# A graph layer on one core: one-hot moved within the step, loads of targets and weights moved back, eight gathers in one group

## The chip, the cores and the metric

The kernel runs on one core of a Trainium2 chip. The metric is the device time of one execution in microseconds (us); less is better. The engines are TensorE (PE, with its weight loads shown as PEld), VectorE (DVE), ScalarE (ACT), GpSimd (POOL) and SyncE (SP). Here SP computes nothing: it issues most of the transfers, one after the other, from one queue. POOL issues the indirect ones.

## The reference, cut to what matters

```python
h = relu(layernorm(x))                        # x: 12500 x 128
msg_src = h @ w_src + b_src;  msg_dst = h @ w_dst
m = msg_src[src] + msg_dst[dst]               # 400000 edges, sorted by dst
rad = silu(silu(edge_attr @ w1 + b1) @ w2 + b2) @ w3 + b3    # 32 -> 64 -> 64 -> 128
m = m * edge_weight * rad
m = (m @ w_sep + b_sep).reshape(E, 8, 32)     # per head: 16 for alpha, 16 for the value
alpha = smooth_leaky_relu(m[:, :, :16]);  value = m[:, :, 16:]
score = einsum('ehk,hk->eh', alpha, alpha_dot)
att = segment_softmax(score, dst)             # over the edges with one target
out = segment_sum(value * att, dst).reshape(12500, 128)
y = x + out @ w_proj + b_proj
```

## The kernel before

**Node phase.** x is loaded in eight transfers. 25 quads of four tiles of 128 rows are then normalised, turned by PE, multiplied with both weight matrices (`products(i)`), copied out of PSUM by ACT (L261, tile `ms`, four buffers) and stored by SP to the tables `t_src` and `t_dst` in HBM (L266). The loop over the quads is written out in order (manual schedule). On SP's queue, between x and the first table store, stand the loads that the later phases need: the targets of all edges as `cur`, 125 rows of 3200 words, and the same shifted by one word as `prev` (L169 to L172); `base`, the first target of each section, in two transfers that repeat one row over the partitions (L176); `ends`, single words, the first and last target of each section (L177); and 14 loads of copies of the small weights in blocks (L188 to L194). 15 more weights are loaded by the helper `load` (L110) from ACT's queue.

At quad 12 `fits()` compares `prev` with `cur` to find out whether the targets are sorted, and from `ends` whether a section of 500 edges spans fewer than 64 targets. After the loop `cuts()` computes a row of marks `same`, where a target differs from the one before, stores it to HBM and makes some small tiles of weights.

**Step phase.** If all fits, `windows()` runs. It takes 1000 edges in a step k, two sections f = 0 and 1 of 500 edges (four tiles of 125). Work on one pair of sections is spread over many steps: loads and gathers run ahead of k, the sums follow in step c = k - 12, and a softmax scan over eight pairs runs once in eight steps. The order of each engine's instructions is the order in which the step's code is written. The parts that the text below speaks of:

- SP's loads: `w_b` (L713, edge weights repeated over 128 partitions), `md` (L719, rows of `t_dst`), `d_b` (L707), `e_t` (L702, edge attributes), the rows for `add_x`; and its stores: `sc_d` (L841, scores), `ob` to the row of `agg` of its window (L924).
- `gather(k, f)`, L739: four indirect transfers, issued by POOL, of 125 rows of `t_src` each, into a tile `gs0` or `gs1` with four buffers. A step issues `gather(k+4, 1)` in its first half and `gather(k+5, 0)` later.
- `prep_make` makes POOL's indices once in 16 steps, `split_md` the parts of md, `add_x` adds x to a chunk of the result in one step of eight.
- `mlp3(k)`: the third matmul of the radial net (L790), then `rad` on DVE (L794).
- `sources(k, f)`: four transposes (L803) of the gathered rows into PSUM (`pm0` or `pm1`).
- `message(k, rad)`: adds `msg_dst` by a one-hot matmul (L811) to `pm`, then mT = (pm + b) * rad on DVE (L816).
- `values(c, f)`: V = mT @ w_v (L901), then pvx = V * Pem, the weights of the softmax, on DVE (L903).
- `alphas(k, f)`: pa = w_a by mT (L820, one PSUM buffer), a sigmoid `sl` on ACT (L822), al = pa * sl on DVE (L824).
- `mlp1(k+2)` (L758), `mlp2(k+1)` (L773): the first two layers of the radial net.
- `sums_begin(c)`: copies the weights beside pvx (ACT), and makes `oh`, the one-hot of each edge's target in its window, on DVE (L888 and L891).
- `sums(c)`: the segment sums as matmuls of `oh` with `pvx` (L912), copied out by ACT as `ob` (L916).
- `e_T` (L749) and `scores` (L831) follow, `scores` in odd steps.

The order of PE's work in a step before: `mlp3(k)`, `sources(k, 1)`, `message(k)`, `values(c, 0)`, `alphas(k, 0)`, `mlp1(k+2)`, `values(c, 1)`, `sources(k+1, 0)`, `alphas(k, 1)`, `mlp2(k+1)`, `sums(c)`, `e_T`, `scores`. The one-hot is issued to DVE at the head of the step, before `rad`.

**The end.** The last 13 steps have only the sums of the pairs still under way. Then parts of windows are scattered, and a final phase multiplies the sums by w_proj and adds x.

Of the kernel before, what the change touches and what calls it, by code (L numbers as in the profile page):

```python
# [30 lines left out]
P = 128  # L31
C = 128
# [24 lines left out]
def gnn_kernel(ctx: ExitStack, tc: tile.TileContext, a: dict, out: bass.AP):  # L57
# [47 lines left out]
    ident = const.tile([P, P], F32, name="ident")  # L105
    make_identity(nc, ident)

    def load(name, shape, ap=None, eng=None):
        t = const.tile(shape, F32, name="c_" + name)
        (eng or nc.scalar).dma_start(out=t, in_=a[name] if ap is None else ap)  # L110
        return t

    eps = const.tile([P, 1], F32, name="eps")
    nc.vector.memset(eps, LN_EPS)
    ones = const.tile([P, P], F32, name="ones")
# [38 lines left out]
    with tc.tile_pool(name="node", bufs=2) as np_, tc.tile_pool(name="node1", bufs=1) as n1, \  # L154
# [9 lines left out]
        dst_r = dst.rearrange("(p c) -> p c", p=RP)  # L164
        cur = n1.tile([RP, RC], I32, name="cur")
        prev = n1.tile([RP, RC], I32, name="prev")
        ends = n1.tile([100, 8, 2], I32, name="ends")
        eb = n1.tile([P, NS, 2], I32, name="eb")
        nc.sync.dma_start(out=cur, in_=dst_r)  # L169
        nc.vector.memset(prev[0:1, 0:1], -1)  # L170
        nc.sync.dma_start(out=prev[0:1, 1:RC], in_=dst_r[0:1, 0:RC - 1])
        nc.sync.dma_start(out=prev[1:RP, :], in_=dst[RC - 1:E - 1].rearrange("(p c) -> p c", c=RC))  # L172
        at = dst[0:1]
        with nc.allow_non_contiguous_dma(reason="the sections' ends"):
            for f in range(2):
                nc.sync.dma_start(out=base[:, f, :], in_=dst_h[f:f + 1, :, 0])  # L176
            nc.sync.dma_start(out=ends, in_=bass.AP(  # L177
                at.tensor, at.offset, [[8 * SEC, 100], [SEC, 8], [SEC - 1, 2]]))
# [6 lines left out]
        for f in range(2):  # L185
            for q in range(2):
                o = (2 * q + f) * RAD
                nc.sync.dma_start(out=w1b[o:o + RAD, f * FC:(f + 1) * FC], in_=a["fc_w1"])  # L188
            s = slice(f * FC, (f + 1) * FC)
            for q in range(2):  # L190
                nc.sync.dma_start(out=w2b[s, q * FC:(q + 1) * FC], in_=a["fc_w2"])
            nc.sync.dma_start(out=w3b[s, :], in_=a["fc_w3"])
            nc.sync.dma_start(out=b12[s, 0:1], in_=a["fc_b1"])
            nc.sync.dma_start(out=b12[s, 1:2], in_=a["fc_b2"])  # L194
        b_n = load("b_n", [C, 1], a["b_src"].rearrange("o c -> c o"))
        dot = load("dot", [C, 1])
        heads = load("heads", [C, C])
        w1, b1 = load("fc_w1", [RAD, FC]), load("fc_b1", [FC, 1])
        w2, b2 = load("fc_w2", [FC, FC]), load("fc_b2", [FC, 1])
        w3, b3 = load("fc_w3", [FC, C]), load("fc_b3", [C, 1])  # L200
        w_a, b_a = load("w_a", [C, C]), load("b_a", [C, 1])
        w_v = load("w_v", [C, C])
        w_proj = load("w_proj", [C, C])
        b_out = load("b_out", [P, C], a["b_proj"].to_broadcast([P, C]))
        b_v = load("b_v", [C, 1])


        mv = n1.tile([P, NB, 2], F32, name="mv")
# [60 lines left out]


        def fits():
            gt = n1.tile([RP, RC], BF16, name="gt")
            nc.vector.tensor_tensor(gt, prev, cur, op=ALU.is_gt)
            cnt = n1.tile([P, 2], F32, name="cnt")
            nc.vector.memset(cnt, 0.0)
            nc.vector.tensor_reduce(cnt[:RP, 0:1], gt, AX.X, ALU.add)
# [24 lines left out]
        v_out = const.tile([P, C], F32, name="v_out")  # L301

        def cuts():
            sm = n1.tile([RP, RC], BF16, name="sm")
            nc.vector.tensor_tensor(sm, prev, cur, op=ALU.not_equal)
            nc.vector.tensor_scalar(sm, sm, RESTART, None, op0=ALU.mult)
            nc.sync.dma_start(out=same[:, 0:E].rearrange("o (p c) -> (o p) c", p=RP), in_=sm)
# [36 lines left out]

    chunks = [(t, min(CH, TPI - t)) for t in range(0, TPI, CH)]
# [310 lines left out]
    def windows():  # L656
# [5 lines left out]
        with tc.tile_pool(name="wk2", bufs=2) as sp, tc.tile_pool(name="ps", bufs=1, space=PSUM) as pp, \  # L662
                tc.manual_schedule(), ExitStack() as held:
            lp = held.enter_context(tc.tile_pool(name="ld", bufs=2))
            prep, e_g, d_g, w_g, md, gath = {}, {}, {}, {}, {}, {}
            eTs, h1s, h2s, ohT, m3, mr, mTs, als, S_all, sms, Ps, Pem, pvx, ohs, accs, xs, Ms, pms = (
                {} for _ in range(18))


            def prep_load(u):  # L670
# [60 lines left out]
                else:  # L731
                    nc.vector.tensor_sub(m3[k][:, 2, :], mr.pop(k), m3[k][:, 1, :])

            def gather(k, f):
                gs = lp.tile([P, TS, C], F32, name=f"gs{f}", bufs=4)
                idx, _ = prep[k // 16]
                for j in range(TS):
                    t = k % 16 * 8 + f * TS + j
# [3 lines left out]
                gath[k, f] = gs  # L742


            def e_T(k):
# [49 lines left out]
                                                   op0=ALU.add, op1=ALU.mult)  # L795
                return rad

            def sources(k, f):

                gs = gath.pop((k, f))  # L800
                pms[k, f] = pp.tile([C, SEC], F32, name=f"pm{f}")
                for t in range(TS):
                    nc.tensor.matmul(pms[k, f][:, t * T:(t + 1) * T], gs[:T, t, :], ident[:T, :T],  # L803
                                     start=(t == 0), stop=False, is_transpose=True, skip_group_check=True)

            def message(k, rad):
                pm = [pms.pop((k, f)) for f in range(2)]
                for j in range(3):
                    for f in range(2):
                        s = slice(f * W, (f + 1) * W)  # L810
# [66 lines left out]
                nc.scalar.copy(Pem[m].rearrange("p t q h -> p t (q h)"), pt)  # L877


            def sums_begin(c):  # L880
                pvx[c] = sp.tile([T, 2, TS, ROW], F32, name="pvx")
                q = c % MP * 2
                for f in range(2):
                    nc.scalar.copy(pvx[c][:, f, :, C:ROW], Pem[c // MP][:, :, q + f, :])
                _, loc = prep[c // 16]
                ohs[c] = sp.tile([T, 8, W], F32, name="oh")
                t0 = c % 16 * 8
# [7 lines left out]

            def values(c, f):
                V = pp.tile([T, TS, C], F32, name="V") if c < NP - LAG else \
                    pp.tile([T, TS, C], F32, name=f"pm{f}")
# [42 lines left out]
            def has(k):  # L941
                return 0 <= k < NP
# [5 lines left out]
            def step(k):  # L948
# [377 lines left out]
```

## Time and profile before

| | before |
|---|---|
| median of three runs | 4723.23 us (4720.04 to 4723.61) |
| the profiled execution | 4712.63 us, span 4710.8 us |
| mean granted TensorE clock | 0.964 |
| busy, PE / PEld / DVE / ACT / POOL | 89% / 50% / 65% / 41% / 67% |
| moved by DMA | 796.36 MB, mean 169 GB/s |

The profile is that of one execution. A row of its groups or waits names a line of the kernel, an engine, an operation and its tiles (out<-in), how often, the busy time and the mean of one in ns, then the idle time just before and who ended it. A row of a timeline gives the start, the duration, engine, line and operation, and in brackets a wait and what ended it. "SPq" is SP's queue, where the time between two issues is shown since SP has no busy time. A row of the view by windows gives a stretch of time, and then for each engine the busy time and the number of instructions in it, the granted clock, the share of the 16 DMA engines that was busy and GB/s.

### The profile page before, as it was taken

Reading aid. Unit: us, or ns where it says so; the run is one execution under the profiler, and the core shown is the slowest. Engines: PE = TensorE matmul, PEld = TensorE weight load, DVE = VectorE, ACT = ScalarE, POOL = GpSimd, SP = SyncE. Lnnn points to the kernel's source line nnn. Section 1 sums busy time; section 2 is a strip of 40 time slices with the busy share of each in tenths; the row PEclk is TensorE's granted clock in tenths of the full one; section 3 lists DMA queues with packets and bytes.
Section 4 is the critical chain, followed back from the end, with each engine's and each line's share of the span. In section 5 each row is a group of like instructions: output and inputs, shape, how many; then the busy total and the mean of one; then the engine's idle time right before and its main releaser. Section 6 shows DMA issues by size and latency. Waiting matters only on the chain.

```text
span 4710.8 us, 88096 instructions
## 1 busy us (share of the span) xinstructions
PE 4212.0 (89%) x29692; PEld 2344.1 (50%) x29692; DVE 3081.2 (65%) x6005; ACT 1921.9 (41%) x4595; POOL 3136.0 (67%) x3223
## 2 busy tenths in 40 slices
PE   4669998999999999999999999999999999999974
PEld 3325554554555555555545555555555555555553
DVE  4436665766766666666666666666666666666666
ACT  3324443443443444443433444444444444444421
POOL 0467776776777777777766777777777767777601
PEclk8779999999999999999999999999999999999987
DMA  4667767777776777777777777777677777777724
GB/s 160 168 162 173 175 167 172 174 178 175 170 176 171 169 176 175 172 178 174 170 175 170 177 174 169 179 172 164 171 174 169 171 168 170 172 168 174 173 64 173
DMA packets 901312, 796.36 MB, mean 169 GB/s; under 512 B 530125, under 2 KB 776829, under 8 KB 900598
## 3 DMA queue, kind: packets, MB, share of 16 engines
q1 hardware_dynamic: 794830, 573.36, 46.8%
q0 software_dynamic: 102816, 210.37, 21.5%
q10 hardware_dynamic: 3202, 6.92, 0.4%
q8 instruction: 234, 3.83, 0.4%
q14 instruction: 230, 1.88, 0.1%
HBM read 649.99 MB, written 140.67 MB: 168 GB/s over the span
## 4 chain that ended last, share of the span: by engine, by line
PE 66%; DVE 10%; DMA 9%; SPq 6%; ACT 5%; issue 4%; POOL 1%; ACTq 0%; POOLq 0%; DVEq 0%
PE pa L820 14%; PE V L901 13%; PE misc L912 7%; PE p L790 6%; PE pm L803 6%; PE pm L811 4%; PE p L758 4%; PE misc L831 4%; PE p L773 4%; DMA md<-t_dst 2%; DMA sc_d<-Sp 2%; PE m L749 2%; ACT sl L822 2%; DMA agg<-ob 2%; DVE al L824 2%
## 5 line engine op out<-in xcount | busy, mean ns | idle before, releaser
L739 POOL DMA_INDIRECT gs<-t_src,idx x3200 | 3121.6, 976 | 1347.2 <-issue 800.8
L822 ACT ACTIVATE sl<-pa,c_b_a 128x500 f32<-128x500 f32 x800 | 541.4, 677 | 1595.5 <-PE pa L820 1594.7
L824 DVE SCALAR_TENSOR_TENSOR al<-pa,sl 128x500 f32<-128x500 f32 x800 | 543.1, 679 | 828.8 <-ACT sl L822 723.6
L820 PE MATMUL pa<-mT,c_w_a 128*128 128x500 f32 x1600 | 851.2, 614 | 244.2 <-DVE mT L816 173.3
L901 PE MATMUL V<-c_w_v,mT 128*125 128x128 f32 x6208 | 895.5, 288 | 0.3
L901 PEld LDWEIGHTS V<-c_w_v,mT 128*125 128x125 f32 x6208 | 746.4, 190 | 290.7 <-issue 176.8
L794 DVE SCALAR_TENSOR_TENSOR rad<-p,c_fc_b,w_b 128x500 f32<-128x500 f32 x800 | 552.9, 733 | 307.2 <-PE p L790 305.7
L903 DVE TENSOR_TENSOR pvx<-V,Pem 125x512 f32<-125x512 f32 x776 | 531.9, 685 | 114.4 <-PE V L901 107.8
L816 DVE SCALAR_TENSOR_TENSOR mT<-pm,c_b_n,rad 128x500 f32<-128x500 f32 x800 | 552.5, 733 | 6.5 <-PE pm L811 6.5
L803 PEld LDWEIGHTS pm<-ident,gs 125*128 125x128 f32 x3200 | 356.7, 142 | 312.8 <-issue 292.3
L803 PE MATMUL pm<-ident,gs 125*128 125x125 f32 x3200 | 505.0, 280 | 7.9 <-DMA gs<-t_src,idx 7.9
L912 PE MATMUL misc<-pvx,oh 125*64 125x136 f32 x6400 | 470.1, 288 | 31.4 <-DVE pvx L903 27.6
L912 PEld LDWEIGHTS misc<-pvx,oh 125*64 125x64 f32 x6400 | 364.5, 138 | 182.9 <-issue 178.6
L790 PE MATMUL p<-h,w3b 64*128 64x500 f32 x1600 | 446.0, 634 | 2.4 <-ACT h L776 2.4
L820 PEld LDWEIGHTS pa<-mT,c_w_a 128*128 128x128 f32 x1600 | 245.0, 193 | 284.5 <-DVE mT L816 195.4
L811 PE MATMUL pm<-ohT,m 64*128 64x500 bf16 x2400 | 323.9, 376 | 0.0
L758 PE MATMUL p<-eT,w1b 64*128 64x250 f32 x1600 | 287.5, 437 | 1.0 <-ACT eT L751 1.0
L725 ACT CAST m<-md 128x128 bf16<-128x128 f32 x400 | 118.3, 296 | 401.1 <-DMA md<-t_dst 400.8
L758 PEld LDWEIGHTS p<-eT,w1b 64*128 64x128 f32 x1600 | 124.7, 191 | 307.5 <-issue 276.3
L761 ACT ACTIVATE h<-p,b 128x500 f32<-128x500 f32 x400 | 272.4, 681 | 4.8 <-PE p L758 4.8
L776 ACT ACTIVATE h<-p,b 128x500 f32<-128x500 f32 x400 | 269.2, 673 | 3.6 <-PE p L773 3.6
L888 DVE TENSOR_TENSOR oh<-lane,loc 125x504 f32<-125x504 f32 x400 | 269.2, 673 | 0.0
(145 smaller groups left out, 3286.1 us busy)
## 6 DMA issues: line engine op xcount, KB each, us to landing
w_b<-in_edge_weight SPq DMA_DIRECT2D x400, 500.0 KB
d_b<-in_dst SPq DMA_DIRECT2D x400, 250.0 KB
gs<-t_src,idx POOLq DMA_INDIRECT x3200
e_t<-in_edge_attr SPq DMA_DIRECT2D x400, 125.0 KB
sc_d<-Sp SPq DMA_DIRECT2D x200, 250.0 KB
win<-ob SPq DMA_DIRECT2D x400, 68.0 KB
agg<-ob SPq DMA_DIRECT2D x800, 33.5 KB
md<-t_dst SPq DMA_DIRECT2D x800, 32.0 KB
```

The lines of the kernel that those rows point to most:

```text
L739: nc.gpsimd.indirect_dma_start(out=gs[:, j, :], out_offset=None, in_=t_src[:, :], in_offset=bass.IndirectOffsetOnAxis(ap=idx[:, t:t + 1], ...
L758: nc.tensor.matmul(p1[:, q, 0:2 * T], w1b[s, :], eTs[k][s, :], start=True, stop=True)
L790: nc.tensor.matmul(p3[:, f, 0:SEC], w3b[s, :], h2s[k][s, :], start=True, stop=True)
L794: nc.vector.scalar_tensor_tensor(rad[:, s], p3[:, f, 0:SEC], b3, w_g[k][:, s], op0=ALU.add, op1=ALU.mult)
L803: nc.tensor.matmul(pms[k, f][:, t * T:(t + 1) * T], gs[:T, t, :], ident[:T, :T], start=(t == 0), stop=False, is_transpose=True, skip_group ...
L816: nc.vector.scalar_tensor_tensor(mTs[k][:, s], pm[f], b_n, rad[:, s], op0=ALU.add, op1=ALU.mult)
L820: nc.tensor.matmul(pa, w_a, mTs[k][:, f * SEC:(f + 1) * SEC], start=True, stop=True)
L822: nc.scalar.activation(sl, pa, AF.Silu, bias=b_a, scale=1.0)
L824: nc.vector.scalar_tensor_tensor(al, pa, 0.25, sl, op0=ALU.mult, op1=ALU.add)
L901: nc.tensor.matmul(V[:, t, :], mTs[c][:, o:o + T], w_v, start=True, stop=True)
L903: nc.vector.tensor_mul(pvx[c][:, f, :, 0:C].rearrange("p t (h k) -> p t h k", h=H), V.rearrange("p t (h k) -> p t h k", h=H), Pem[c // MP] ...
L912: nc.tensor.matmul(acc[f * W:(f + 1) * W, :], ohs[c][:, f * TS + t, :], pvx[c][:, f, t, :], start=(t == 0), stop=(t == TS - 1), skip_group ...
```

## The change

It has four parts.

1. *Loads of targets and weights.* The helper `load` goes; all 29 weight loads are issued by SP in `load_weights`, and the targets in `load_targets`. Both stand after `products(1)` in the loop over the quads. `cur` becomes one tile of 128 rows of 3126 words: 3125 targets of the row and, in column 0, the last target of the row before, fetched by a transfer of 127 single words. `prev` goes, and `fits` and `cuts` compare two shifted views of `cur`.
2. *`cuts`* is issued at quad 20 rather than after the loop.
3. *Gathers and transposes.* One tile `gs` holds all eight gathers of a pair, with four buffers, issued by `gather(k+4)` at the head of the step. `sources` goes: its eight transposes stand in `message`, which comes after `mlp3`. The tiles `pm0` and `pm1` become two buffers of `pm`.
4. *The one-hot.* `sums_begin(c)` is split: `weights(c)` stays at its place, `one_hot(c)` stands after `values(c, 1)`.

```diff
-    def load(name, shape, ap=None, eng=None):
-        t = const.tile(shape, F32, name="c_" + name)
-        (eng or nc.scalar).dma_start(out=t, in_=a[name] if ap is None else ap)
-        return t
...
-        cur = n1.tile([RP, RC], I32, name="cur")
-        prev = n1.tile([RP, RC], I32, name="prev")
...
+        cur = n1.tile([P, CC + 1], I32, name="cur")
+        nc.vector.memset(cur[0:1, 0:1], -1)
...
+        def load_targets():
+            nc.sync.dma_start(out=cur[:, 1:CC + 1], in_=dst.rearrange("(p c) -> p c", p=P))
+            at = dst[CC - 1:CC]
+            with nc.allow_non_contiguous_dma(reason="single targets"):
+                nc.sync.dma_start(out=cur[1:P, 0:1], in_=bass.AP(at.tensor, at.offset, [[CC, P - 1], [1, 1]]))
+                for f in range(2):
+                    nc.sync.dma_start(out=base[:, f, :], in_=dst_h[f:f + 1, :, 0])
+                at = dst[0:1]
+                nc.sync.dma_start(out=ends, in_=bass.AP(
+                    at.tensor, at.offset, [[8 * SEC, 100], [SEC, 8], [SEC - 1, 2]]))
+
+        def load_weights():
+            for name, t in wt.items():
+                ap = a[name]
...
+                nc.sync.dma_start(out=t, in_=ap)
+            for f in range(2):
...
...
-            nc.vector.tensor_tensor(gt, prev, cur, op=ALU.is_gt)
+            nc.vector.tensor_tensor(gt, cur[:, 0:CC], cur[:, 1:CC + 1], op=ALU.is_gt)
...
             products(i)
+            if i == 1:
+                load_targets()
+                load_weights()
             if i == 12:
                 fits()
-        cuts()
+            if i == 20:
+                cuts()
...
-            def gather(k, f):
-                gs = lp.tile([P, TS, C], F32, name=f"gs{f}", bufs=4)
+            def gather(k):
+                gs = lp.tile([P, 8, C], F32, name="gs", bufs=4)
...
             def message(k, rad):
-                pm = [pms.pop((k, f)) for f in range(2)]
+                gs = gath[k]
+                pm = [pp.tile([C, SEC], F32, name="pm", bufs=2) for _ in range(2)]
+                for f in range(2):
+                    for t in range(TS):
+                        nc.tensor.matmul(pm[f][:, t * T:(t + 1) * T], gs[:T, f * TS + t, :], ...)
...
+                if has(k + 4):
+                    gather(k + 4)
                 if has(k + 1):
                     split_md(k + 1, 0)
                 if has(c):
-                    sums_begin(c)
-                rad = mlp3(k) if has(k) else None
+                    weights(c)
                 if has(k):
-                    sources(k, 1)
-                if has(k + 4):
-                    gather(k + 4, 1)
-                if has(k):
-                    message(k, rad)
+                    message(k, mlp3(k))
                 if has(c):
                     values(c, 0)
...
                 if has(c):
                     values(c, 1)
-
-                if has(k + 1):
-                    sources(k + 1, 0)
-                if has(k + 5):
-                    gather(k + 5, 0)
+                    one_hot(c)
                 if has(k):
                     alphas(k, 1)
```

More of the change, by code (lines that the diff above doesn't have):

```diff
@@ L163, in gnn_kernel @@
         nc.sync.dma_start(out=x_all[:tail, NF, :], in_=x[NF * P:, :])
-        dst_r = dst.rearrange("(p c) -> p c", p=RP)
-        cur = n1.tile([RP, RC], I32, name="cur")
-        prev = n1.tile([RP, RC], I32, name="prev")
[L167 to L178, printed above, removed]
         w1b = const.tile([P, P], F32, name="w1b")
@@ L184, in gnn_kernel @@
         b12 = const.tile([P, 2], F32, name="b12")
[L185 to L204, printed above, removed]
@@ L205, in gnn_kernel @@
-        b_v = load("b_v", [C, 1])
+        CC = E // P
+        cur = n1.tile([P, CC + 1], I32, name="cur")
+        nc.vector.memset(cur[0:1, 0:1], -1)
+        ends = n1.tile([100, 8, 2], I32, name="ends")
+        eb = n1.tile([P, NS, 2], I32, name="eb")
+        wt = {name: const.tile(shape, F32, name="c_" + name) for name, shape in (
+            ("b_src", [C, 1]), ("dot", [C, 1]), ("heads", [C, C]), ("fc_w1", [RAD, FC]), ("fc_b1", [FC, 1]),
+            ("fc_w2", [FC, FC]), ("fc_b2", [FC, 1]), ("fc_w3", [FC, C]), ("fc_b3", [C, 1]), ("w_a", [C, C]),
+            ("b_a", [C, 1]), ("w_v", [C, C]), ("w_proj", [C, C]), ("b_proj", [P, C]), ("b_v", [C, 1]))}
@@ new lines, in gnn_kernel @@
+        b_n, dot, heads, w1, b1, w2, b2, w3, b3, w_a, b_a, w_v, w_proj, b_out, b_v = wt.values()
+        def load_targets():
[8 more added lines that the diff above has]
+                    at.tensor, at.offset, [[8 * SEC, 100], [SEC, 8], [SEC - 1, 2]]))
@@ new lines, in load_weights @@
+        def load_weights():
+            for name, t in wt.items():
+                ap = a[name]
+                if name == "b_src":
+                    ap = ap.rearrange("o c -> c o")
+                elif name == "b_proj":
+                    ap = ap.to_broadcast([P, C])
+                nc.sync.dma_start(out=t, in_=ap)
+            for f in range(2):
+                for q in range(2):
+                    o = (2 * q + f) * RAD
+                    nc.sync.dma_start(out=w1b[o:o + RAD, f * FC:(f + 1) * FC], in_=a["fc_w1"])
+                s = slice(f * FC, (f + 1) * FC)
+                for q in range(2):
+                    nc.sync.dma_start(out=w2b[s, q * FC:(q + 1) * FC], in_=a["fc_w2"])
+                nc.sync.dma_start(out=w3b[s, :], in_=a["fc_w3"])
+                nc.sync.dma_start(out=b12[s, 0:1], in_=a["fc_b1"])
+                nc.sync.dma_start(out=b12[s, 1:2], in_=a["fc_b2"])
@@ L271, in fits @@
         def fits():
-            gt = n1.tile([RP, RC], BF16, name="gt")
-            nc.vector.tensor_tensor(gt, prev, cur, op=ALU.is_gt)
+            gt = n1.tile([P, CC], BF16, name="gt")
+            nc.vector.tensor_tensor(gt, cur[:, 0:CC], cur[:, 1:CC + 1], op=ALU.is_gt)
             cnt = n1.tile([P, 2], F32, name="cnt")
             nc.vector.memset(cnt, 0.0)
-            nc.vector.tensor_reduce(cnt[:RP, 0:1], gt, AX.X, ALU.add)
+            nc.vector.tensor_reduce(cnt[:, 0:1], gt, AX.X, ALU.add)
             span = n1.tile([100, 8], F32, name="span")
@@ L303, in cuts @@
         def cuts():
-            sm = n1.tile([RP, RC], BF16, name="sm")
-            nc.vector.tensor_tensor(sm, prev, cur, op=ALU.not_equal)
+            sm = n1.tile([P, CC], BF16, name="sm")
+            nc.vector.tensor_tensor(sm, cur[:, 0:CC], cur[:, 1:CC + 1], op=ALU.not_equal)
             nc.vector.tensor_scalar(sm, sm, RESTART, None, op0=ALU.mult)
-            nc.sync.dma_start(out=same[:, 0:E].rearrange("o (p c) -> (o p) c", p=RP), in_=sm)
+            nc.sync.dma_start(out=same[:, 0:E].rearrange("o (p c) -> (o p) c", p=P), in_=sm)
             nc.sync.dma_start(out=same[:, E:E + 1], in_=sm[0:1, 0:1])
@@ L665, in windows @@
             prep, e_g, d_g, w_g, md, gath = {}, {}, {}, {}, {}, {}
-            eTs, h1s, h2s, ohT, m3, mr, mTs, als, S_all, sms, Ps, Pem, pvx, ohs, accs, xs, Ms, pms = (
-                {} for _ in range(18))
+            eTs, h1s, h2s, ohT, m3, mr, mTs, als, S_all, sms, Ps, Pem, pvx, ohs, accs, xs, Ms = (
+                {} for _ in range(17))
             def prep_load(u):
@@ L732, in split_md @@
                     nc.vector.tensor_sub(m3[k][:, 2, :], mr.pop(k), m3[k][:, 1, :])
-            def gather(k, f):
-                gs = lp.tile([P, TS, C], F32, name=f"gs{f}", bufs=4)
+            def gather(k):
+                gs = lp.tile([P, 8, C], F32, name="gs", bufs=4)
                 idx, _ = prep[k // 16]
-                for j in range(TS):
-                    t = k % 16 * 8 + f * TS + j
+                for j in range(8):
+                    t = k % 16 * 8 + j
                     nc.gpsimd.indirect_dma_start(
@@ L741, in gather @@
                         in_offset=bass.IndirectOffsetOnAxis(ap=idx[:, t:t + 1], axis=0))
-                gath[k, f] = gs
+                gath[k] = gs
             def e_T(k):
@@ L796, in mlp3 @@
                 return rad
[L798 to L804, printed above, removed]
-            def message(k, rad):
-                pm = [pms.pop((k, f)) for f in range(2)]
+            def message(k, rad):
+                gs = gath[k]
+                pm = [pp.tile([C, SEC], F32, name="pm", bufs=2) for _ in range(2)]
+                for f in range(2):
+                    for t in range(TS):
+                        nc.tensor.matmul(pm[f][:, t * T:(t + 1) * T], gs[:T, f * TS + t, :],
+                                         ident[:T, :T], start=(t == 0), stop=False,
+                                         is_transpose=True, skip_group_check=True)
                 for j in range(3):
@@ L877, in softmax_T, with weights @@
                 nc.scalar.copy(Pem[m].rearrange("p t q h -> p t (q h)"), pt)
-            def sums_begin(c):
+            def weights(c):
                 pvx[c] = sp.tile([T, 2, TS, ROW], F32, name="pvx")
@@ L884, in sums_begin, with one_hot @@
                     nc.scalar.copy(pvx[c][:, f, :, C:ROW], Pem[c // MP][:, :, q + f, :])
+            def one_hot(c):
                 _, loc = prep[c // 16]
@@ L897, in values @@
                 V = pp.tile([T, TS, C], F32, name="V") if c < NP - LAG else \
-                    pp.tile([T, TS, C], F32, name=f"pm{f}")
+                    pp.tile([T, TS, C], F32, name="pm", bufs=2)
                 for t in range(TS):
```

## The prediction

> **What bounds the kernel now.** I read the page first: busy shares and the chain that ended last.
>
> ```profile
> PE 4212.0 (89%) x29692; PEld 2344.1 (50%) x29692; DVE 3081.2 (65%) x6005; ACT 1921.9 (41%) x4595; POOL 3136.0 (67%) x3223
> ...
> PE 66%; DVE 10%; DMA 9%; SPq 6%; ACT 5%; issue 4%; POOL 1%; ACTq 0%; POOLq 0%; DVEq 0%
> ```
>
> This looks like a TensorE kernel with a little VectorE lateness. The page leaves SyncE out, so the second view is SP's own waits, from 500 to 4400 us:
>
> ```profile
> SPq L924 <- DMA agg<-ob: 124.3, 200, 2.1
> SPq L841 <- DMA sc_d<-Sp: 120.4, 44, 4.4
> SPq L702 <- PE pm L803: 22.3, 49, 0.7
> ```
>
> SP waits for its own stores to land and next to nothing else; no wait on a compute engine is longer than 1.2 us. In that window it issues 362 loads of w_b, the first at 504.0 and the last at 4393.6 us (source view of L713): 3889.6 / 361 = 10.78 us per step, 10.66 in the last third. It never catches up with the others. The third view, PE's timeline, shows what PE would need:
>
> ```profile
> 1514.84 1.11 PE L790 MATMUL p<-h,w3b 64*128 64x500 f32 x4
> ...
> 1524.12 1.11 PE L790 MATMUL p<-h,w3b 64*128 64x500 f32 x4
> ...
> 1548.59 1.11 PE L820 MATMUL pa<-mT,c_w_a 128*128 128x500 f32 x2 [1.37 <-DVE mT L816]
> ...
> 1552.51 1.11 PE L820 MATMUL pa<-mT,c_w_a 128*128 128x500 f32 x2 [0.70 <-DVE al L824]
> ```
>
> A step without stalls is 9.28 us, or 10.33 with `scores` (1524.12 to 1534.45); the step after each softmax scan, which holds the two stalls above, is 14.27 (1543.73 to 1558.00). Eight steps are 4 x 9.28 + 3 x 10.33 + 14.27 = 82.4, with half of a `prep_make` (1.3 us in 16 steps) 83.0: 10.38 a step, stalls included. SP's 10.78 is slower. POOL needs 8 gathers of 0.976 plus gaps near 0.28, 10.0 us. So in mid-kernel SP sets the pace, and PE's other waits (`add_x` waiting for its rows, ACT waiting for md) are how PE is held to it.
>
> The head of the kernel is different. SP's timeline, then ACT's:
>
> ```profile
> 19.81 13.10 SPq L176 DMA_DIRECT2D base<-in_dst  x2
> 32.95 13.82 SPq L177 DMA_DIRECT2D ends<-in_dst  x1
> 46.89 15.71 SPq L188 DMA_DIRECT2D w1b<-in_fc_w  x2
> ...
> 70.05 0.52 SPq L266 DMA_DIRECT2D t_src<-ms  x1
> ```
>
> ```profile
> 73.29 0.58 ACT L261 COPY ms<-pm 128x512 f32<-128x512 f32 x1 [34.57 <-DMA t_dst<-ms]
> ```
>
> The table stores stand behind the loads of targets and weights; the four ms buffers are full, so ACT idles 34.6 us and PE with it. The view by windows shows why these loads are slow:
>
> ```profile
> 18.00:24.00 6.00, 5.29 (x14) 3.42 (x14) 4.92 (x23) 2.95 (x9) 0.00 (x0) 1.00 1.01 412
> ...
> 30.00:36.00 6.00, 4.96 (x23) 3.71 (x24) 4.18 (x18) 5.09 (x12) 0.00 (x0) 1.00 0.34 126
> ```
>
> The last two columns are DMA share and GB/s. x (128 rows) fills the DMA engines; once cur (125 rows) and prev (124 rows) are left, a third of them works, 0.28 from 36 to 48 us.
>
> **The change part by part, against the profiled execution's 4712.6 us.** The median shown is 4723.2, so I carry the difference over to that.
>
> *The head's loads.* ACT loses 15 loads. Its first `rstd` at 15.83 stood behind them; its input was ready at 7.61, so with the table load of 1.28 it starts at about 8.9, 6.9 us sooner. `products(1)` was copied out at 28.1, now near 21.2, and its stores are issued by 22.1. Then SP takes `load_targets` and `load_weights`, with `products(2)` and everything later queued behind them. Their issues: cur 0.3; the 127 single words like rb's 128 words, 0.64; base twice its first row of 2.5 us, 5.0; ends with 1600 words at the 6.3 ns per word of that row, 10.1; the 15 weights at ACT's rows (0.33 to 1.01), 8.3; the other 14 at 0.59, 8.0. Sum 32.3, so the third table store goes at 54.4, not 70.05, with two quads stored before it. Two quads are 6.9 us (ACT copies 73.29 to 80.21). Gain 15.7 + 6.9 = 22.6.
>
> Here a rule is weighed. The measured row is cur and prev at a share of 0.34 then 0.28. The Trainium skill (DMA: Bandwidth & Descriptors, section "Why a DMA increments its semaphore by 16 and not by 1") says that a DMA runs on the largest number of engines up to 16 that divides the slowest dimension. That gives 5 for 125 rows, 4 for 124 and 16 for 128, and the shares fit 5/16 and 4/16. No row shows the new cur; by the rule it drains like x, 1.6 MB at 412 GB/s, 4 us. But the rule speaks against the new 127 words: 127 is prime, so one engine takes them all. By rb's row they cost 0.64 us; by the rule a FIFO of 127 words on one engine, fewer than the 160 that ends puts on each of its ten. I keep 0.64 and leave 4 us for it in the range. The other bound of the whole block: if the words, not the rows, were slow, L176 to L188's first issue stays at 42 us and the gain falls to about -4; if words cost nothing it is 36.
>
> The same page (section "Issuing engines are not separate DMA queues") says that a second issuing engine saves only sequencer time. By that, moving 15 loads from ACT to SP is nearly free; by ACT's rows it is 8.3 us of SP time on the path, which I charge.
>
> *`cuts` at i == 20.* At the end it cost 142.2 to 150.5 on DVE and held the next phase until its 125-row store had landed: SP's first load of the step phase is at 155.0, where the last table stores alone would give 149. That returns 6 us. Inside the loop it costs like `fits`, whose 7.3 us of DVE stopped PE for 8.6; here 8, less 1.5 caught up as no stats are left. Net 0.5 lost. Node phase: -22.
>
> *Gathers.* The number, order and queue of the indirect DMAs stay. With four buffers, gs(k+4) takes the place of gs(k), which `message(k)` still reads; so though written at the head, the eight gathers wait for its eight transposes, some 2.2 us into the step. POOL's 10.0 us then fit into 10.78, and rows are ready three steps early. Behind them POOL has only more gathers. 0 us; without that slack, 16 us for each 0.04 us of overrun per step.
>
> *Transposes and one-hot.* Four transposes (0.43 us of PE) move from mid-step to the head, the one-hot (0.68 + 0.17, 0.76 overlapped) from before rad to after the second pvx. mT comes 0.8 earlier where DVE is late, and PE arrives 0.58 later, so the stall of 1.37 vanishes. But pa has one buffer: between the two `alphas` PE now has 1.6 us of work, not 2.1. In a clean step al ends 2.46 after the first pa starts and PE arrives at 2.56: no wait. After a table load (1.28) the 0.70 becomes 1.13. Net 0.54 gained in each of 50 steps, 27 us, if PE set the pace. `sums` now waits for the one-hot: pvx ends at 1521.62 in the step I followed, the one-hot 0.7 later at 1522.3, PE would arrive at 1522.25: 0.1 per step, 40 us if exposed. PE needs (82.4 - 0.5 + 0.65) / 8 = 10.31 plus 0.1. SP's pace of 10.66 to 10.78 covers both, so I book 0. SP's own queue in the steps is untouched, its registers and stores too.
>
> *The last steps* (from 4513 us) have no loads, so no cover:
>
> ```profile
> 4515.29 0.42 PE L912 MATMUL misc<-pvx,oh 125*64 125x136 f32 x2
> 4516.16 1.11 PE L912 MATMUL misc<-pvx,oh 125*64 125x136 f32 x14 [0.46 <-DVE pvx L903]
> ```
>
> The one-hot was done beside `values`; now it follows pvx, and no pair of `sums` starts early: about +1.2 in the first three such steps and +0.5 in three later ones, where DVE isn't the bound already. +5.
>
> Sum: -22 + 0 + 5 = -17; 4712.6 becomes 4695.6, the median 4706.
>
> **The rivals.**
> 1. *The head isn't shortened* (single words as slow as cur's rows were): node about 0, tail +5, 4728. For it: issues of words took 10 to 15 us. Against: the share of 0.28 says few engines, not many words.
> 2. *PE becomes the bound at `sums`*, the slower side. It decides once the wait for the one-hot and the second pa passes 10.66 - 10.31 = 0.35 us a step. At 0.5 it costs 0.15 x 390 = 58 us: 4764. For it: the margins are tenths, and a stalled PE also loses its early weight loads. Against: 0.1 by the rows.
> 3. *SP was not the bound* and DVE lateness was (173 us of PE waiting for mT in the waits view): 27 us in the scan steps, 24 `add_x` steps x 1.3 and 20 late steps x 1.1, together 80: 4626. Against: SP's unbroken queue.
> 4. *Nothing moves the gathers*: that part doesn't do what it says, as told, and costs nothing either way.
>
> **How the numbers follow.** Likeliest (0.60): 4690 to 4720. Rival 1 (0.14): 4720 to 4735. Rival 2 (0.14): 4735 to 4800. Rival 3 (0.12): 4600 to 4670. A measurement of this kernel tells about 0.2% from no change, 9.4 us, so faster is below 4713.8. That is 0.49 of the likeliest and rival 3: 0.61. Same: 0.11 of the likeliest and 0.09 of rival 1: 0.20. Slower: the rest of rival 1 and rival 2: 0.19. The range 4672 to 4740 leaves out rival 3 and most of rival 2.
>
> **What would show it.** Right: ACT's stall in the node phase is under 20 us and the first w_b load comes near 141, not 162.7; the pace of w_b stays within 10.7 to 10.85; PE's waits for mT shrink while those for md and xs grow; `sums` waits for oh by about 0.1. Wrong: the third table store after 65 us; a w_b pace above 10.9 with SP waiting on ACT's ob (rival 2), or below 10.6 (rival 3); POOL without any wait for pm.

## The result, and the profile after

| | before | after |
|---|---|---|
| median of four runs | 4722.19 us (4720.04 to 4723.61) | 4681.99 us (4677.24 to 4688.59) |
| the profiled execution | 4712.63 us, span 4710.8 us | 4684.59 us, span 4682.8 us |
| mean granted TensorE clock, profiled | 0.964 | 0.966 |

The ratio is 0.9917, 95% interval 0.9902 to 0.9933: 40 us less, by the interval 32 to 46. The forecast was 4706 in a range of 4672 to 4740. The two profiled executions are only 28 us apart: that of before is 9.6 us under its median, that of after 2.6 us above. The stages below account for the 28; the other 12 lie between executions and can be put in no stage.

The page of the changed kernel, busy shares and the chain that ended last:

```profile
PE 4234.1 (90%) x29692; PEld 2353.3 (50%) x29692; DVE 3103.2 (66%) x6005; ACT 1924.4 (41%) x4595; POOL 3203.9 (68%) x3223
...
PE 70%; DMA 9%; SPq 7%; ACT 5%; DVE 5%; issue 3%; POOL 1%; ACTq 0%; POOLq 0%; DVEq 0%
```

VectorE's share of the chain has halved, from 10% to 5%, and TensorE's has grown from 66% to 70%; where the time was won the chain does not tell. Two points in time divide the span in three: the first and last matmul of `mlp3`, in the source view of its line, before and then after (duration min/median/max, then first and last start):

```profile
L790 PE MATMUL p<-h,w3b x1600: 578/682/1200, 171.1 to 4504.4; 64*128 64x500 f32 x178
```

```profile
L794 PE MATMUL p<-h,w3b x1600: 579/683/1200, 138.9 to 4475.0; 64*128 64x500 f32 x178
```

Ahead of the steps: 171.1 - 138.9 = 32.2 us gained. The 400 steps: 4333.3 before, 4336.1 after, 2.8 lost. From there to the end of the span: 206.4 before, 207.8 after, 1.4 lost. Together 28.0.

**The head.** SP's timeline after, and one row of ACT's:

```profile
20.64 0.45 SPq L178 DMA_DIRECT2D cur<-in_dst  x1
21.14 0.32 SPq L181 DMA_DIRECT2D cur<-in_dst  x1
21.50 6.52 SPq L183 DMA_DIRECT2D base<-in_dst  x2
28.06 0.92 SPq L185 DMA_DIRECT2D ends<-in_dst  x1
...
46.58 0.51 SPq L266 DMA_DIRECT2D t_src<-ms  x1
```

```profile
49.81 1.07 ACT L261 COPY ms<-pm 128x512 f32<-128x512 f32 x2 [12.59 <-DMA t_dst<-ms]
```

The 127 single words are the second row, 0.32 us; `ends` needs 0.92 us where it took 13.82. The whole block of loads lasts 25.9 us (20.64 to 46.58), so the table stores go on at 46.58 with two quads stored before the block, where the first store of all went at 70.05, and ACT stands 12.6 us, not 34.6.

**The steps.** TensorE's waits from 500 to 4380 us, before and then after (line, who was waited for, us in total, times, longest):

```profile
PE pa L820 <- DVE mT L816: 148.1, 76, 9.7
PE pa L820 <- DVE al L824: 42.5, 58, 2.6
```

```profile
PE pa L822 <- DVE mT L818: 87.7, 32, 9.2
PE pa L822 <- DVE al L826: 70.4, 71, 2.3
```

These waits fall from 190.6 us (148.1 + 42.5) to 158.1 (87.7 + 70.4), 32.5 us less. Two more groups of TensorE in the same window, the transposes of the gathered rows and `sums`, before and then after; the last number is the idle time before them:

```profile
L803 PE MATMUL pm<-ident,gs 125*128 125x125 f32 x2876 | 448.4, 278 | 0.0
L912 PE MATMUL misc<-pvx,oh 125*64 125x136 f32 x5760 | 415.0, 286 | 0.0
```

```profile
L916 PE MATMUL misc<-pvx,oh 125*64 125x136 f32 x5760 | 414.0, 286 | 0.3
...
L807 PE MATMUL pm<-ident,gs 125*128 125x125 f32 x2872 | 385.9, 277 | 0.0
```

So in the steps `sums` does not stand still for the late one-hot. On the page of after, over the whole span, it has 37.7 us of waiting for it. All of this lies in the last steps (window 4380 to 4720, after):

```profile
L916 PE MATMUL misc<-pvx,oh 125*64 125x136 f32 x356 | 29.2, 311 | 37.7 <-DVE oh L895 37.7
```

Before, `sums` waits 31.4 us there, 27.6 of them for pvx.

TensorE waits 32 us less, and yet the 400 steps are 2.8 us longer. The starts of `mlp3` show why. Each list starts with the step after a softmax scan; then comes a clean step:

```profile
1976.71 1.11 PE L790 MATMUL p<-h,w3b 64*128 64x500 f32 x4
...
1990.74 1.11 PE L790 MATMUL p<-h,w3b 64*128 64x500 f32 x4
...
2000.01 1.11 PE L790 MATMUL p<-h,w3b 64*128 64x500 f32 x4
```

```profile
1767.04 1.11 PE L794 MATMUL p<-h,w3b 64*128 64x500 f32 x4
...
1780.35 1.11 PE L794 MATMUL p<-h,w3b 64*128 64x500 f32 x4
...
1789.73 1.11 PE L794 MATMUL p<-h,w3b 64*128 64x500 f32 x4
```

Before, these two steps take 14.03 and 9.27 us; after, 13.31 and 9.38. A step with `scores` takes 10.33 before and 10.43 after. The medians of all such steps through the middle of the kernel are 14.03 and 9.28 before, 13.31 and 9.38 after. An estimate from them: 50 steps after a scan are 0.72 us shorter each, 36 us in all, and the other 350 are 0.10 longer, 35 us in all. The change both gains and loses in the steps, and the two cancel.

About half of the 0.10 is the one-hot, for which the first weight load of `sums` (PEld, loading while other matmuls run) now waits:

```profile
2314.35 0.89 PEld L916 LDWEIGHTS misc<-pvx,oh 125*64 125x64 f32 x16 [0.42 <-DVE oh L895]
```

It starts 0.63 us after the first matmul of `mlp2` (2313.72), and 0.59 us after it before (1511.04 and 1510.45). The other half lies in the second `alphas`, which starts 0.99 us ahead of `mlp2` (2312.73), and 0.93 before (1509.52).

POOL's gathers, which the prediction held at 0.976 us, take 0.997 (page of after): with a gap of 0.305 after each (waits view of POOL: 810.2 us in 2654 gaps) that is 10.4 us of a 10.8 us step. TensorE's transposes did not wait for the gathered rows in that window, as the 0.0 of L803 and L807 shows.

### The profile page after: what moved, and what is told of

Same layout as the page of the kernel before. It is cut to its first block, busy times and chain, and to the rows that moved or that the text cites. A ratio compares the mean times of both kernels' runs of the same rounds, so it can differ in the third digit from the quotient of the medians.

```text
span 4682.8 us, 87683 instructions
## 1 busy us (share of the span) xinstructions
PE 4234.1 (90%) x29692; PEld 2353.3 (50%) x29692; DVE 3103.2 (66%) x6005; ACT 1924.4 (41%) x4595; POOL 3203.9 (68%) x3223
## 4 chain that ended last, share of the span: by engine, by line
PE 70%; DMA 9%; SPq 7%; ACT 5%; DVE 5%; issue 3%; POOL 1%; ACTq 0%; POOLq 0%; DVEq 0%
PE pa L822 14%; PE V L905 13%; PE misc L916 8%; PE p L794 7%; PE pm L807 7%; PE pm L813 5%; PE p L777 4%; PE p L762 4%; PE misc L833 4%; DMA agg<-ob 3%; SPq L928 2%; DMA md<-t_dst 2%; PE m L753 2%; DMA sc_d<-Sp 2%; ACT L824 1%
## 5 line engine op out<-in xcount | busy, mean ns | idle before, releaser
L743 POOL DMA_INDIRECT gs<-t_src,idx x3200 | 3189.5, 997 | 1256.7 <-issue 899.7
L822 PE MATMUL pa<-mT,c_w_a 128*128 128x500 f32 x1600 | 871.1, 627 | 212.1 <-DVE mT L818 107.8
L818 DVE SCALAR_TENSOR_TENSOR mT<-pm,c_b_src,rad 128x500 f32<-128x500 f32 x800 | 552.8, 733 | 117.2 <-PE pm L813 115.7
L916 PE MATMUL misc<-pvx,oh 125*64 125x136 f32 x6400 | 463.4, 287 | 38.0 <-DVE oh L895 37.7
L807 PEld LDWEIGHTS pm<-ident,gs 125*128 125x128 f32 x3200 | 339.3, 141 | 302.0 <-issue 262.7
L916 PEld LDWEIGHTS misc<-pvx,oh 125*64 125x64 f32 x6400 | 361.2, 137 | 200.5 <-DVE oh L895 158.1
L807 PE MATMUL pm<-ident,gs 125*128 125x125 f32 x3200 | 433.3, 279 | 2.4 <-DMA gs<-t_src,idx 2.2
L777 PE MATMUL p<-h,w2b 64*64 64x250 f32 x3200 | 265.5, 403 | 5.0 <-ACT h L765 5.0
```

Of the source, the lines that this page charges most:

```text
L743: nc.gpsimd.indirect_dma_start(out=gs[:, j, :], out_offset=None, in_=t_src[:, :], in_offset=bass.IndirectOffsetOnAxis(ap=idx[:, t:t + 1], ...
L807: nc.tensor.matmul(pm[f][:, t * T:(t + 1) * T], gs[:T, f * TS + t, :], ident[:T, :T], start=(t == 0), stop=False, is_transpose=True, skip_ ...
L818: nc.vector.scalar_tensor_tensor(mTs[k][:, s], pm[f], b_n, rad[:, s], op0=ALU.add, op1=ALU.mult)
L822: nc.tensor.matmul(pa, w_a, mTs[k][:, f * SEC:(f + 1) * SEC], start=True, stop=True)
L916: nc.tensor.matmul(acc[f * W:(f + 1) * W, :], ohs[c][:, f * TS + t, :], pvx[c][:, f, t, :], start=(t == 0), stop=(t == TS - 1), skip_group ...
```

## The experiments

All twelve ran on other Trainium2 chips, where the kernel before took 6.02 to 6.17 ms. A ratio is always against the kernel before on the same chip. The stretch ahead of the steps takes the same there as in the first profiles, within 2.2 us (first load of w_b at 129.3 to 130.7 us with the changed head, 129.9 in the profile after; 164.9 with the old one, 162.7 in the profile before), so it is read from the traces. The changed kernel itself was not run there; cuts_end, which differs from it in the place of `cuts` alone, stands nearest. The steps are paced by something else there, and tell what the parts do when the cover that the prediction counted on is gone.

| run | head | cuts | gathers | transposes | one-hot | ratio (95%) | clock | first w_b, us |
|---|---|---|---|---|---|---|---|---|
| before (first chip) | old | end | two groups | two places | early | | 0.964 | 162.7 |
| after (first chip) | new | in loop | one group | one place | late | 0.9917 | 0.966 | 129.9 |
| rows128_in_place | 128 rows only | end | two | two | early | 0.996 (0.9926 to 0.9994) | 0.884 | 126.1 |
| head_only | new | in loop | two | two | early | 0.9919 (0.9882 to 0.9957) | 0.875 | 129.7 |
| head_cuts_end | new | end | two | two | early | 0.9933 (0.9896 to 0.997) | 0.879 | 124.3 |
| step_only | old | end | one | one | late | 1.156 (1.1503 to 1.1618) | 0.808 | 164.9 |
| cuts_end (one execution) | new | end | one | one | late | 1.159 | 0.804 | 124.8 |
| onehot_back | new | in loop | one | one | early | 1.1591 (1.1521 to 1.166) | 0.821 | 130.2 |
| gathers_back | new | in loop | two | two | late | 0.9502 (0.9445 to 0.9558) | 0.896 | 130.7 |
| gathers_head | new | in loop | one | two | late | 1.1456 (1.1392 to 1.1521) | 0.808 | 130.5 |
| gs5 | new | in loop | one, 5 buffers | one | late | 1.1354 (1.1309 to 1.1399) | 0.826 | 129.3 |
| best | new | end | two | two | late | 0.9581 (0.9539 to 0.9623) | 0.899 | 123.8 |
| before_relief | old | end | two | two | early | 1.0255 (1.0205 to 1.0305) | 0.865 | 152.6, by ACT |
| after_relief | new | in loop | one | one | late | 1.1423 (1.1366 to 1.1481) | 0.815 | 120.4, by ACT |

The clock is the mean granted TensorE clock of the profiled execution.

**head_only and step_only: the change in its two halves.** The first is the file after up to the step phase with the steps of before; the second the reverse.

> The kernel before with parts 1 and 2 of the change (targets and weights loaded after products(1), cur in 128 rows, cuts at quad 20); gathers, transposes and one-hot stay as before. Theory A (the whole gain lies ahead of the steps, and SP's queue sets the pace of the steps): 32 us less than before in the trace at the first load of w_b, and 28 to 40 us less in time, the same as the whole change. Theory B (the steps gained too, and the trace of the one profiled execution hides it behind its own luck): 15 to 25 us less.

> The kernel before with parts 3 and 4 of the change alone (gathers of a pair at the head of the step, transposes in message, one-hot after the second pvx). Theory A: within 5 us of before, though PE waits less for mT and more for al and oh, since SP's queue paces the steps. Theory B: 10 to 20 us less. If the last steps lose what was forecast: 5 us more.

Measured: the head alone 0.9919, about 50 us (26 to 73) less, its first w_b 33.0 us earlier than in the profile before (35.2 earlier than in step_only, on its own chip): theory A's 28 to 40 lies inside. The steps alone: 1.156, some 950 us more, which neither theory had. By the first chip's traces the changed steps cost the kernel 3 us; here they cost a sixth of its time.

**rows128_in_place: how many rows, or where in the queue?**

```diff
-        cur = n1.tile([RP, RC], I32, name="cur")       # 125 rows
-        prev = n1.tile([RP, RC], I32, name="prev")
-        nc.sync.dma_start(out=cur, in_=dst_r)
-        nc.sync.dma_start(out=prev[1:RP, :], ...)
+        cur = n1.tile([P, CC + 1], I32, name="cur")    # 128 rows, same place in the queue
+        nc.sync.dma_start(out=cur[:, 1:CC + 1], ...)
+        nc.sync.dma_start(out=cur[1:P, 0:1], ...)      # 127 single words
```

> The kernel before with only cur changed: one tile of 128 rows with the 127 single words, no prev, at its old place in SP's queue ahead of all table stores; weights on ACT and cuts after the loop as before. If the number of rows is what made the loads ahead of the stores slow[...]: the third table store, at 70 us before, goes 18 to 25 us sooner and the time falls by about 20 us. If the single words are slow, or if the place in the queue is what counts: under 6 us.

SP's timeline of this kernel:

```profile
40.27 0.52 SPq L266 DMA_DIRECT2D t_src<-ms  x1
...
117.53 0.29 SPq L308 DMA_DIRECT2D same<-sm  x1
117.97 0.34 SPq L674 DMA_DIRECT2D ri<-in_src  x1
```

The first table store (the expectation calls it the third) goes at 40.27 us instead of 70.05, and the first load of w_b at 126.1 instead of 162.7: 36.6 us, more than the whole changed head gives (33.0). The edit does two things, though: the rows become 128, and without `prev` half the words are loaded. No run parts the two. The view by windows of this kernel speaks for the rows:

```profile
26.00:28.00 2.00, 2.00 (x13) 1.74 (x13) 1.86 (x10) 2.00 (x6) 0.00 (x0) 1.00 0.98 404
```

The DMA engines are full (share 0.98, 404 GB/s) until x and cur are in, at about 28 us; the next 2 us have a share of 0.44. In the kernel before they work at a share of 0.25 to 0.37 and at 77 to 134 GB/s from 26 to 46 us. An estimate from these rates: cur and prev together (3.2 MB) would take some 8 us at 404 GB/s, where more than 20 us pass before, so most of the gain belongs to the rows.

The last two rows of SP's timeline show a second effect of the 128 rows: before, 7.6 us lay between the marks' store (147.39) and the next load (155.00), now 0.44. Ratio 0.996: 24 us less, 4 to 45 by the interval; the 36.6 are inside.

**cuts_end and head_cuts_end: what does `cuts` inside the loop return?** Both have this edit, the second with the steps of before:

```diff
-            if i == 20:
-                cuts()
+        cuts()
```

> The changed kernel with cuts after the loop again, as before. If cuts at quad 20 returned the wait for the marks' store (6 us) and cost 0.5 in the loop, the first load of w_b comes 5 us later than the changed kernel's 129.9 us; if the stop inside the loop costs what it saves, within 1 us. What it does to the steps: nothing, by every theory.

> The changed head with the steps of before, and cuts after the loop. If the marks' store of 128 rows no longer holds up the next loads, as the trace of the changed kernel with cuts at the end showed (first load of w_b 124.8 us, with cuts in the loop 129.9), it beats the new head alone by 5 us: first w_b near 125, ratio to before 0.991. If the wait for that store comes back with the steps of before: w_b near 135, ratio 0.993.

SP's timeline, cuts after the loop with the changed kernel and then the changed kernel itself:

```profile
124.80 0.60 SPq L716 DMA_DIRECT2D w_b<-in_edge_weight  x1
```

```profile
129.91 0.60 SPq L717 DMA_DIRECT2D w_b<-in_edge_weight  x1
```

The expectation of cuts_end was wrong in sign: put back, it comes 5.1 us earlier, and with the steps of before 5.4 (129.7 to 124.3). Inside the loop `cuts` stops the quads: in the changed kernel TensorE stands 6.65 us before the first matmul of `cuts`, at 109.24. After the loop, with 128 rows, the next load follows its store by 0.44 us. The times of head_only and head_cuts_end don't tell 5 us of 6100 apart. rows128_in_place at 126.1 and head_cuts_end at 124.3 also give the price of the other edits: later loads and all weights on SP bring 1.8 us, no more than the 2.2 us by which traces of one head differ between chips.

**onehot_back, gathers_back and gathers_head: which part of the steps costs 950 us?**

```diff
                 if has(c):
                     weights(c)
+                    one_hot(c)           # onehot_back; no longer after values(c, 1)
```

gathers_back has `gather(k, f)` and `sources(k, f)` of before. gathers_head has the one `gather(k+4)` at the head of the step and the tile of eight, with the transposes in two places:

```diff
+                if has(k + 4):
+                    gather(k + 4)
...
-                if has(k + 4):
-                    gather(k + 4, 1)
...
-                if has(k + 5):
-                    gather(k + 5, 0)
```

> The changed kernel with the one-hot at its old place, at the head of the step before rad; gathers and transposes stay as changed. On a chip where the changed steps cost some 950 us: if the wait of sums for the late one-hot is what costs it (the rival that named this wait), the time falls to within 60 us of the kernel with the new head alone, ratio near 0.99 to the kernel before. If the transposes taken out of mid-step cost it (no PE work left that covers alphas' one PSUM buffer, mlp2 and sums), it stays 800 us above, ratio 1.13 to 1.16. On a chip where SP paces the steps: within 5 us of the changed kernel.

> The changed kernel with gathers and transposes of four in two places as before, the one-hot late as changed. The mirror of the kernel with the one-hot put back: if the one-hot costs the 950 us, ratio 1.13 to 1.16; if the transposes cost it, near 0.99. If each costs a part, both lie between and the parts add up to about 950 us.

> New head and late one-hot; the eight gathers of a pair in one tile, issued at the head of the step as changed, but the transposes in two places as before (four in mid-step for the next pair, four after mlp3). It splits the 16% that gathers and transposes cost together on these chips. If the transposes' place costs it: ratio 0.94 to 0.96, as with both put back. If the gathers' place and buffers cost it (all eight wait for the last transpose of the pair four steps back): 1.10 or more.

With the one-hot put back nothing changes (1.159, as in cuts_end). With gathers and transposes put back the ratio is 0.950: the late one-hot alone, against head_only's 0.992, is worth about 4% here, some 250 us; beside the gathers in one group it is worth nothing (step_only 1.156, onehot_back 1.159). gathers_back and gathers_head differ only in the gathers (one tile of eight, issued together at the head of the step; or two tiles of four, issued apart, one of them a step further ahead), and are 0.950 and 1.146. So neither transposes nor one-hot cost it; the gathers in one group do, whether by their tile, its buffers or their place.

**gs5: is it the wait for the buffers?** `bufs=4` becomes `bufs=5` for `gs`.

> The changed kernel with five buffers of gs instead of four, so that the eight gathers at the head of a step need not wait for that step's own transposes; nothing else differs. If that wait is what costs 15% on these chips (the gathers start 2 to 3 us into the step, run 10 us, and PE's results come only when they have landed): ratio 0.95 to 1.0. If the eight gathers in one run cost it, whenever they start: 1.13 to 1.16. By the prediction's own step (the wait for the transposes costs nothing): no change to the changed kernel, 1.15 here.

POOL's waits from 500 to 4380 us in gathers_head and gs5:

```profile
POOL gs L743 <- PE pm L807: 1628.8, 230, 12.4
```

```profile
POOL gs L743 <- PE pm L807: 1466.2, 214, 10.8
```

1.135, the expectation's second case. A fifth buffer brings 1 to 2%, but the wait hardly falls (it is 750.1 us in best, with two groups): POOL, done with eight gathers in 10 us of a longer step, can only run one step further ahead and wait there. So this run did not take the wait away and does not settle it. In every version with one group the gathers start right behind a step's transposes.

What the traces show of the lost time is TensorE's results coming late. The last step of the radial net's second layer and the activation that needs it, in the changed kernel's profile and in cuts_end:

```profile
2313.72 0.65 PE L777 MATMUL p<-h,w2b 64*64 64x250 f32 x8
2314.44 0.68 ACT L780 ACTIVATE h<-p,b 128x500 f32<-128x500 f32 x1
```

```profile
2302.06 0.65 PE L776 MATMUL p<-h,w2b 64*64 64x250 f32 x8
...
2305.95 0.94 POOL L742 DMA_INDIRECT gs<-t_src,idx  x1 [0.30 <-issue]
2308.68 0.68 ACT L779 ACTIVATE h<-p,b 128x500 f32<-128x500 f32 x1 [4.30 <-remote]
2309.41 2.04 PE L793 MATMUL p<-h,w3b 64*128 64x500 f32 x4 [4.29 <-ACT h L779]
```

There the activation follows 0.07 us after the recorded end of the matmuls, here 5.97 us, 1.8 us after the group's last gather has been issued ("remote": nothing in the trace releases it). TensorE then idles, and the next `mlp3` runs for 2.04 us against 1.11, at a granted clock of 0.50 (view by windows, 2308 to 2312). The mean granted clock agrees, 0.80 to 0.83 in all versions with one group, 0.86 to 0.90 in all with two. The kernel before, with two groups, is itself 26 to 32% slower there than on the first chip, so the lateness is not the one group's alone. Why TensorE's results come late on these chips, and whether the gathers cause it or only fall on the same time, stays open: no run takes one away without the other.

**before_relief and after_relief: does SP set the pace of the steps?**

```diff
-                nc.sync.dma_start(out=w_g[k], in_=ew_p[:, k, :].to_broadcast([P, PR]))
+                nc.scalar.dma_start(out=w_g[k], in_=ew_p[:, k, :].to_broadcast([P, PR]))
-                nc.sync.dma_start(out=win[c * P:(c + 1) * P, :], in_=accs[c])
+                nc.scalar.dma_start(out=win[c * P:(c + 1) * P, :], in_=accs[c])
```

> The kernel before with two transfers of each step, the load of w_b and the store of win, issued by ACT instead of SP: the same bytes, 0.38 + 0.45 us and the gaps beside them less on SP's queue, 0.9 us a step. Theory A (SP's issue time is the pace): the pace falls from 10.78 to what PE needs by its stall-free steps, 10.4, so 100 to 150 us less. Theory C (the time of the transfers in the DMA engines is the pace, SP only shows it): 0 to 20 us less. Theory D (PE and DVE set the pace): 0, or slower by ACT's extra 0.8 us a step where it is late.

> The changed kernel with the same two transfers on ACT. With SP off the path, its distance to the kernel before with the same two transfers on ACT is what gathers, transposes and one-hot are worth to PE, beside the 32 us of the head. If the shorter waits for mT count (the rival of 80 us): 100 us or more apart. If the wait for the one-hot and the single pa buffer count: under 30 us apart, or the other way. Theory A says little here beyond 32 with some 0 to 30 more either way; theory C says 28 to 40 apart, and both near their own versions without the move.

before_relief: 1.0255 (1.0205 to 1.0305), some 155 us more, theory D's case. after_relief: 1.1423 (1.1366 to 1.1481), 1.4 points below step_only on the same chip, of which the new head alone is 0.8: the move brings next to nothing, and with it the changed kernel stays 12 points above before_relief, "the other way" of the expectation. SP is not the pace on these chips; its waits in head_only, from 500 to 4380 us, say why:

```profile
SPq L840 <- ACT m L729: 927.0, 124, 11.6
```

There SP waits for ACT; in the first profiles no wait of SP on a compute engine was longer than 1.6 us. So the theory that SP sets the pace was not tested where it was made, and falls only here. For the first chip a rival is POOL, which the prediction put at 10.0 us a step: it needs 10.25 before (8 x (0.976 + 0.305)) and 10.4 after. But there TensorE's transposes waited 0.0 us for gathered rows from 500 to 4380 us, which speaks against POOL.

**best: what the runs point to.** The changed head with `cuts()` after the loop, the one-hot late, gathers and transposes as before.

> New head, cuts after the loop, one-hot late, gathers and transposes as before: what the runs so far point to. First load of w_b near 125 us (with cuts in the loop 130), and a ratio of 0.949 to 0.950, 5 us under the kernel with gathers and transposes put back, which this measurement may not tell apart. If cuts in the loop was of use to the steps after all: 0.952 or more.

0.9581, first w_b at 123.8. Against the kernel before on the same chip it is some 260 us faster. The ratio lies above the 0.949 to 0.950 expected, in the range named for `cuts` in the loop being of use after all. But gathers_back's 0.9502 is from another chip, and the intervals overlap (0.9539 to 0.9623, 0.9445 to 0.9558): the 5 us of `cuts` show in the trace, and the times do not decide. Neither was run on a chip of the first kind, so what they would give there is not measured.

## Why the prediction was right, point by point

The direction and the range held. The likeliest case was less than half the measured gain, and 4682 lies in a gap, from 4670 to 4690, to which the prediction's cases gave no chance. The head carries the gain, as forecast; the zero of the steps came by luck of two terms that cancel.

*The head's loads.* Forecast 22.6, measured 30.4: ACT restarts at 49.81 instead of 73.29 (23.5 us) with two quads more behind it (6.9, as forecast). The mis-sized term is `ends`: 10.1 us, 0.92 measured. Its price per word came from the first row of base, 2.52 us for 400 words. That row was itself held up: after, the first row of base takes 5.87, until cur is in, and the second 0.61. The 13.82 us of `ends` before were the queue held up behind cur and prev too, for in rows128_in_place, at the same place, it takes 0.91. base was 6.52 against 5.0, the 15 weights 9.3 against 8.3 (29.03 to 38.33, so their move to SP was not nearly free), the rest near its rows, and the block began at 20.64 instead of 22.1. The rule weighed there, a DMA's engines as the largest number up to 16 that divides the rows (the Trainium skill, DMA: Bandwidth & Descriptors, "Why a DMA increments its semaphore by 16 and not by 1"), agrees with rows128_in_place: a DMA share of 0.98 while cur comes in as 128 rows, 0.25 to 0.37 with 125 and 124. The 127 words, against which it spoke, took 0.32 us to issue, and no wait of their own is seen: the row behind them ends at 27.4, about when cur is in (113 GB/s from 26 to 28 us, 2 from 28 to 30).

*`cuts` at quad 20.* Forecast: 0.5 lost inside the loop, 6 returned. The 6 us were real (7.6 to 0.44), but the 128 rows return them, not the move: the move itself loses 5.1 to 5.4 us. The step that failed is putting one gain down to the wrong edit of two. The sum was saved by the other terms: -32 against -22.

*Transposes and one-hot.* Both came out, in full. The step after a scan is 0.72 us shorter (forecast 0.54), 36 us in 50 of them (forecast 27). The clean step is 0.10 longer, as forecast, but only half of that is the one-hot; the other half is the second `alphas`, where the working had found no wait. Together 36 - 35, beside 2.8 us lost in the steps. The rest lies in steps that vary, those with `add_x` above all.

*Steps: 0 booked, 2.8 lost.* The number was right and the reason was not shown. SP's pace was to cover what TensorE wins or loses, 40 us lost only "if exposed"; the clean steps show the 0.10 exposed. Since the two terms cancel, no run here tells whether a net gain would have been covered. The row on which the reason rested cannot tell either: SP issues one load of w_b per step, so the spacing of 10.78 us is the length of the step (4333.3 / 400 = 10.83), whichever engine is slowest. Waits for SP's loads did grow, as the prediction said they would, from 500 to 4380 us: those of `add_x` (VectorE) for its rows from 74.9 us in 17 waits to 101.1 in 23, those of ACT for md from 286.8 to 362.7. So loads do hold up some steps, but not the clean ones.

Rival 3's 80 us did not come, but its premise, that SP is not the bound, is not refuted: its 27 us of the scan steps were there and more, and the clean steps ate them. Rival 2's wait of `sums` came at 0.05 us a step, not at 0.5.

*Gathers: 0 booked, "costs nothing either way" (rival 4).* On the first chip nothing speaks against it: POOL's rows grow by 0.02 us and TensorE does not wait for them. But the price without slack was put at an overrun of POOL, and the runs show another: 17 to 21% where TensorE's results come late (onehot_back against head_only: 1.1591 / 0.9919 = 1.17; gathers_head against gathers_back: 1.1456 / 0.9502 = 1.21), with POOL waiting some 40% of the time (1628.8 of 3880 us in gathers_head). It is the largest effect in the runs and had no term in the working; the first chip does not show it.

*The last steps.* Forecast 5 lost, measured 1.4 from the last `mlp3` to the end; `sums` itself waits 6.6 us longer there (31.4 to 38.0).

## What to carry to other kernels

A transfer that looks slow in a queue may only stand behind another: before its row is used as a price, look for what drains ahead of it. Here one tile of 128 rows in place of two of 125 and 124 was worth 36.6 us, and the whole reordered head with it 33. The spacing of a load that is issued once per step is the length of the step and does not show that its queue sets it; the lengths of single kinds of steps, side by side, show what a change does to each. And two edits that share one gain must be run apart: `cuts` in the loop loses 5 us behind a head that gained 33, and the gathers of eight lose 17 to 21% on the other chips, while the one-hot, beside gathers of four, gains 4%.

## What was not expected of the hardware

The same kernel took 4.72 ms on one chip and 5.97 to 6.22 ms on the chips of the experiments, in every run there. Ahead of the steps the traces agree within 2.2 us; in the steps an engine starts up to 6 us after the recorded end of the TensorE work it needs, where 0.07 us was seen on the first chip, and the mean granted clock falls from 0.96 to between 0.80 and 0.90. The order of the steps, worth 2.8 us on the first chip, is worth a sixth of the time or more on the others. The cause stays open.
